# Pacing VectorE's side work in attention, and respacing scatters and gathers between expert blocks

## The chip, the cores and the metric

The kernel runs on one core of one Trainium2 chip, in fp32. The metric is the device time of one execution in microseconds, lower being better; a figure for a kernel is the median of its runs. The engines are called TensorE (PE; its weight loads are listed apart as PEld), VectorE (DVE), ScalarE (ACT), GpSimd (POOL) and SyncE (SP, which here only issues DMAs).

## The reference, cut to what matters

The input is a pair of images, 2 × 256 channels × 56 × 56 pixels, so 3136 tokens of 256 values in each batch. Layer 0 is a non-local convolution block without a softmax (a product of linear maps, folded into one 256 × 256 matrix), with a residual and a ReLU. Layer 1 is a transformer layer over the tokens:

```python
t = _to_tokens(x)
t = t + _L1_attn_ref(_ln_t(t), L1_attn_W_attn, L1_attn_W_proj)
t = t + _L1_ffn_ref(_ln_t(t), L1_ffn_gate_w, L1_ffn_gate_b, ...)
x = _from_tokens(t, x)
```

`_L1_attn_ref` is causal softmax attention with four heads of 64. `_L1_ffn_ref` sends every token to the best two of eight experts; an expert is 256 → 512, exact GELU, 512 → 256, and its output is weighted with the softmax value of the gate:

```python
top2_vals, top2_idx = jax.lax.top_k(probs, 2)
...
h = jax.nn.gelu(xf @ w1 + bb1, approximate=False)
y = h @ w2 + bb2
return (acc + we[:, None] * y, None)
```

## The kernel before

In time the kernel has four stages, which follow one another with some overlap: the convolution, attention of batch 0, attention of batch 1, and the expert blocks. Each engine works through its own list of instructions in the order in which the Python code issues them, so the order is written out by hand.

**Attention (`attend`).** A query block has W = 448 tokens; there are NB = 7 of them in a batch, and `hp` counts two pairs of heads. One step (b, i, hp, j) is one tile of 128 keys against a query block: scores on TensorE (L804), exp on ScalarE (L808) into a tile `st`, a mask on VectorE where the tile is cut by the diagonal (L811), and the sum of the exps on VectorE (L822, L827) into `acc`. The product of the exps with the values (L855) follows LAG = 3 steps later. After the last step of a query block ScalarE copies the finished product (L862) and POOL adds its two halves into `qT` (L863).

Two steps after that comes a *visit*. It issues the projections of the next queries, keys and values (L599, L613, L628), and the output projection of finished rows with its residual (`project_out`, L682 and L687). Then `sum_rows` (L866 to L890) turns the collected exps into row sums: eight matmuls (L876), a copy on ScalarE (L881) into `line`, and SP's DMAs (L884, L887) to memory and back. A list `later` of tasks with due steps holds what follows: `invert` 4 steps later (reciprocal L896 and DMAs L897, L902), `scale` 6 steps after that (L908, which multiplies the rows in `qT`), `hand_on` 2 steps after that.

All the rest of the work is cut into generators in a queue: the statistics of the second layer norm (`closer`, L177 and L178), the routing arithmetic, and the scatter of each token's normalized row to the slots of its two experts (copies L1493 and, for batch 1, L1499 on VectorE, then the indirect DMA L1501 on POOL, two per tile of 128 tokens). Within attention `between` (L2162) takes one piece from that queue in every step, except in the cut steps of the first query block:

```python
tick[0] += 1
if not cut or i:
    pull()
```

**Experts (`experts`).** There are 102 blocks of 128 rows. One turn of the loop issues: `hidden` (L1637 on TensorE, GELU L1646 on ScalarE), `inputs` of a later block (transposes L1614), `weights` (a copy of the expert's first matrix on VectorE, L1625), `outputs` of the block three earlier (L1656 on TensorE, L1666 on VectorE, then a DMA to `y_slots` L1671 or a scatter to `y_tokens` on POOL L1677), and last `between`, which is `meanwhile` (L2234). Every third turn the experts' numbers are read into registers of TensorE and VectorE (`experts_of`, L1517 to L1523). The first 57 blocks hold the rows of batch 0, the last of these mixed with rows of batch 1.

`meanwhile` counts turns and pulls pieces from the queue: 2 or 3 by turns while batch 1's scatters are being issued (`placed[1]` and not `sent[1]`), otherwise 4 or 2. When batch 0's outputs are complete, `written` (L2220) is called once: it makes three iota tiles on POOL (L2227) and queues `finish(0)` and `finish(1)`. `finish(0)` collects batch 0's result: two outputs per token from `y_slots` by indirect DMAs on POOL (L1834), added on VectorE (L1869), transposed on TensorE (L1883), copied on ScalarE (L1888) and stored (L1889). Its gathers are limited to 1 or 2 a turn:

```python
while gathered[0] == 1 + turn[0] % 2:
    yield False
```

Of the kernel before, what the change touches and what calls it, by code (L numbers as in the profile page):

```python
# [28 lines left out]
def conv_attn_moe_kernel(  # L29
# [481 lines left out]
    def layer1(nm, general):  # L511

        with ExitStack() as whole:
# [182 lines left out]
                    yield False  # L696

            unclosed = [NCH] * B

            def closer(b, first, m, k):  # L700

                for n in range(first, first + m):
                    stats(b, n, 1, k, bg, f"o{nm}{b}")
                    unclosed[b] -= 1
                    yield True

            def attend(qT, kT, v, fst, fs, psc, py, open_batch, visit, between, clock, later, finished):
# [156 lines left out]
                        del yps[b, hp, i]  # L864

                def sum_rows(b, hp, i):  # L866
                    yh = qT[:, hp, i * W : (i + 1) * W]
                    r = (b * NH + hp) * NB + i
                    sn = f"{nm}{b}_{hp}_{i}"
                    acc = accs[b, hp, i]  # L870
                    summed.add((b, hp, i))
                    sp = bank(f"sp_{b}_{hp}_{i}")

                    flat = acc.rearrange("p a w -> p (a w)")
                    for g in range(4):
                        nc.tensor.matmul(  # L876
                            sp[g * 32 : (g + 1) * 32, : W // 2], ones[:, :32],
                            flat[:, g * W // 2 : (g + 1) * W // 2], start=True, stop=True,
                        )
                    line = fs.tile([P, W], F32, tag="rb", bufs=3, name=f"line_{sn}")  # L880
                    nc.scalar.copy(line[:, : W // 2], sp[:, : W // 2])  # L881
                    halves = sum_d[r].rearrange("a (h w) -> (a h) w", h=2)
                    for g in range(4):
                        nc.sync.dma_start(  # L884
                            out=halves[g : g + 1], in_=line[g * 32 : g * 32 + 1, : W // 2]
                        )
                    nc.sync.dma_start(  # L887
                        out=sums[:, r], in_=sum_d[r].rearrange("a (p f) -> (a p) f", p=HS)
                    )
                    later.append((clock[0] + 4, invert, b, hp, i, yh))  # L890

                def invert(b, hp, i, yh):
                    r = (b * NH + hp) * NB + i
                    sn = f"{nm}{b}_{hp}_{i}"
                    back = fs.tile([P, 2 * W // P], F32, tag="back", name=f"back_{sn}")
                    nc.vector.reciprocal(back, sums[:, r])  # L896
                    nc.sync.dma_start(  # L897
                        out=inv_d[r].rearrange("a (p f) -> (a p) f", p=HS), in_=back
                    )
                    rb = fs.tile([P, W], F32, tag="rb", bufs=3, name=f"rb_{sn}")  # L900
                    for a in range(2):
                        nc.sync.dma_start(  # L902
                            out=rb[a * HS : (a + 1) * HS], in_=inv_d[r, a].partition_broadcast(HS)
                        )
                    later.append((clock[0] + 6, partial(scale, rb), b, hp, i, yh))

                def scale(rb, b, hp, i, yh):
                    nc.vector.tensor_tensor(yh, yh, rb, ALU.mult)  # L908
                    later.append((clock[0] + 2, hand_on, b, hp, i, yh))

                def hand_on(b, hp, i, yh):
# [2 lines left out]
                def due(now):  # L914
                    while later and (now is None or later[0][0] <= now):
                        _, task, b, hp, i, yh = later.pop(0)
                        task(b, hp, i, yh)
                        later.sort(key=lambda e: e[0])

                ends = {s[:2]: n for n, s in enumerate(steps)}  # L920
                LAG, BEHIND, FREED = 3, 2, 4
                visits = {BEHIND: (0, -1, NH - 1)}
# [4 lines left out]
                final = visits.pop(len(steps) + BEHIND)  # L927
                visits[len(steps) + 1] = final
                for n in range(len(steps) + LAG):
                    if n in visits:  # L930
                        visit(*visits[n])
                        b, i, hp = visits[n]
                        if i >= 0 and visits[n] != final:
                            sum_rows(b, hp, i)
                        aligned()
                    if n + 1 < len(steps) and n > LAG and steps[n][2] == 0 and steps[n - LAG - 1][2] == 0 and steps[n - LAG - 1][4]:
                        turn_rows(*steps[n][:2])
                    if n < len(steps):
                        b, i = steps[n][:2]
                        if n == 0 or steps[n - 1][0] != b:  # L940
                            open_batch(b)
                        between(b, i, ends[b, i] - n, (steps[n][3] + 1) * P > i * W + 1)

                    late = n >= LAG and steps[n - LAG][4]
                    if n >= LAG:
                        due(clock[0])
                        clock[0] += 1
                    if n >= LAG and not late:
                        values(n - LAG)
                    if n < len(steps):  # L950
                        scores(n)
                    if late:
                        values(n - LAG)
                sum_rows(final[0], final[2], final[1])
                return due

            def attend_general(b, qT, kT, v):
# [584 lines left out]
            def experts(w1s, w2s, b2s, ex, es, ps6, between, need, written, settle, decide):  # L1542


                LATE = 3
# [230 lines left out]
                for n in range(-1, MAIN + 1):  # L1776
# [11 lines left out]
                    for m in (n + 1, n + 2):  # L1788
                        if m < MAIN and m not in wb:
                            wb[m] = weights(m)  # L1790
                    if n == MAIN - 1:
                        decide()
                    for m in sorted(act):
# [18 lines left out]
                        ids.extend(experts_of(len(ids) // GB))  # L1812
                    between()

            def finish(b, oy, bufs):

                t = ts[b]

                def fetch(n, m, k):
# [8 lines left out]
                    ahead.append((n, m, k, ys, rows))  # L1828
                    for c, y in enumerate(ys):
                        for a in range(m):  # L1830
                            while gathered[0] == 1 + turn[0] % 2:
                                yield False
                            gathered[0] += 1
                            nc.gpsimd.indirect_dma_start(  # L1834
                                out=y[:k, a],
                                out_offset=None,
                                in_=y_slots,
                                in_offset=bass.IndirectOffsetOnAxis(
                                    ap=idxs[b][:k, c, n + a : n + a + 1], axis=0
                                ),  # L1840
                                bounds_check=MIXED * P - 1,
                                oob_is_err=False,
                            )
                            yield True
# [46 lines left out]
                        in_=ot[:, :, :w],  # L1891
                    )

                ahead, added = deque(), None
                parts = deque(pairs())
                if b:
                    parts = deque([(0, 1, P), *pairs(1, LAST)])
                while b == 0 and (parts or ahead):
                    if parts:
                        yield from fetch(*parts.popleft())  # L1900
                    if len(ahead) == bufs or not parts:
                        now = ahead.popleft()
                        yield from add(*now)
# [182 lines left out]
            else:  # L2086
# [54 lines left out]
                def visit(b, i, hp):  # L2141
# [20 lines left out]
                def between(b, i, left, cut):  # L2162
# [33 lines left out]
            with ExitStack() as moe:  # L2196
# [23 lines left out]
                def written():  # L2220
# [4 lines left out]
                    for a in range(GB):  # L2225
                        hots.append(hot.tile([P, REST], F32, name=f"hot{a}_{nm}"))
                        nc.gpsimd.iota(  # L2227
                            hots[a], pattern=[[1, REST]], base=LAST * P - OFF, channel_multiplier=0,
                            allow_small_or_imprecise_dtypes=True,
                        )  # L2230
# [25 lines left out]
                with tc.manual_schedule(engines={PE, DVE, POOL, SP, ACT}):  # L2256
                    experts(
                        first[0], w2s, b2s, ex, es, ps6,
                        meanwhile, need, written, settle, decide,
                    )  # L2260

    def late():
# [170 lines left out]
```

## Time and profile before

| | |
|---|---|
| three runs | 1254.31, 1254.82, 1254.89 us |
| median | 1254.82 us |
| the profiled execution | 1272.23 us, of which its span 1270.5 us |
| granted TensorE clock over the span | 0.995 |
| convolution | 0 to about 112 us |
| attention, batch 0 | about 112 to 470 us |
| attention, batch 1 | about 470 to 845 us |
| expert blocks | about 845 to 1271 us |

The profile was recorded in an execution of its own, 17.4 us longer than the median. Durations and positions below come from it. "Busy" is the time in which an engine executes an instruction; "issue" as a releaser means that the engine waited for nothing that the profile shows. VectorE's busy share over the span, in 40 slices from first to last, in tenths:

```profile
DVE  2683567566766575576677887785743433455664
```

It is highest in slices 19 to 28, which is attention of batch 1.

### The profile page before, as it was taken

The numbers are of one execution on the slowest core, as the hardware profiler recorded it, in microseconds if no ns is written. First come the engines' busy times: TensorE is split into PE (matmuls) and PEld (weight loads), VectorE is DVE, ScalarE is ACT, GpSimd is POOL, SyncE is SP. The second block draws the span as 40 slices with busy tenths as digits, with TensorE's granted clock in tenths as the row PEclk, the third lists the DMA queues.
The fourth block names the chain that finished last, engine by engine and source line by source line (L and its number), as shares of the span: only waits on it lengthen the run. The fifth ranks groups of instructions, "written<-read, shape, count | busy, mean of one in ns | idle before, by whom it ended". The sixth has DMA issues, their size and how long they took to land.

```text
span 1270.5 us, 28742 instructions
## 1 busy us (share of the span) xinstructions
PE 1247.3 (98%) x10881; PEld 857.1 (67%) x10881; DVE 773.9 (61%) x1687; ACT 613.1 (48%) x1237; POOL 356.2 (28%) x318
## 2 busy tenths in 40 slices
PE   8999999999999999999999999999999999999998
PEld 8876655555454645655555543469888999899996
DVE  2683567566766575576677887785743433455664
ACT  0255555565656565455555655563332333344442
POOL 1103231110021104211112766100266112666651
PEclk9999999999999999999999999999999999999999
DMA  9995101000000000100000223641344343466654
GB/s 314 354 345 187 25 23 37 25 15 26 14 17 16 7 20 17 36 21 14 9 16 25 71 67 110 202 136 61 101 135 151 101 114 101 142 200 200 212 164 125
DMA packets 118723, 125.66 MB, mean 99 GB/s; under 512 B 27223, under 2 KB 108488, under 8 KB 118578
## 3 DMA queue, kind: packets, MB, share of 16 engines
q1 hardware_dynamic: 107922, 97.19, 25.3%
q0 software_dynamic: 9840, 25.67, 6.0%
q8 instruction: 90, 1.47, 0.5%
q10 hardware_dynamic: 816, 0.88, 0.2%
q14 instruction: 55, 0.45, 0.1%
HBM read 62.06 MB, written 61.05 MB: 97 GB/s over the span
## 4 chain that ended last, share of the span: by engine, by line
PE 91%; DVE 4%; DMA 1%; issue 1%; ACT 1%; SPq 0%; DVEq 0%; ACTq 0%
PE sc_f L804 19%; PE yp_f L855 18%; PE ht_f L1637 14%; PE yp_f L1656 14%; PE qk_f L613 7%; PE v_f L628 4%; PE pp_f L682 3%; PE cp L410 3%; PE gram L317 2%; DVE acc_f L827 2%; PE tp_f L1614 2%; PE sp_f L876 1%; PE xp_f L599 1%; PE yo_f L1883 1%; DMA w1s_f<-in_w_dram 0%
## 5 line engine op out<-in xcount | busy, mean ns | idle before, releaser
L808 ACT ACTIVATE st_f<-sc_f 128x896 f32<-128x896 f32 (+5 forms) x400 | 330.7, 838 | 198.0 <-PE sc_f L804 178.9
L827 DVE TENSOR_TENSOR acc_f<-acc_f,st_f 128x896 f32<-128x896 f32 (+6 forms) x344 | 344.5, 1002 | 118.9 <-ACT st_f L808 109.1
L804 PE MATMUL sc_f<-qT_f,kT_f 64*64 64x448 f32 (+5 forms) x3136 | 347.5, 499 | 0.3 <-ACT st_f L808 0.3
L855 PE MATMUL yp_f<-st_f,v_f 64*64 64x448 f32 (+5 forms) x2928 | 328.0, 510 | 4.1 <-ACT acc_f L862 2.5
L804 PEld LDWEIGHTS sc_f<-qT_f,kT_f 64*64 64x64 f32 x3136 | 144.8, 133 | 128.9 <-issue 106.2
L1646 ACT ACTIVATE g_f<-ht_f,b1b 128x128 f32<-128x128 f32 x408 | 116.6, 371 | 227.3 <-PE ht_f L1637 123.4
L855 PEld LDWEIGHTS yp_f<-st_f,v_f 64*64 64x64 f32 x2928 | 125.1, 133 | 132.2 <-issue 99.3
L1637 PE MATMUL ht_f<-xT_f,w_f 128*128 128x128 f32 x1600 | 196.9, 276 | 5.2 <-issue 5.2
L1637 PEld LDWEIGHTS ht_f<-xT_f,w_f 128*128 128x128 f32 x1600 | 193.8, 192 | 9.1 <-issue 4.6
L1501 POOL DMA_INDIRECT x_slots<-xr_f,idx x100 | 120.4, 1204 | 147.0 <-DVE xr_f L1499 77.6
L863 POOL TENSOR_TENSOR qT_f<-acc_f 128x448 f32<-128x448 f32 x26 | 29.6, 1140 | 406.3 <-ACT acc_f L862 406.3
L1625 DVE COPY w_f<-w1s_f 128x1024 f32 x102 | 72.7, 713 | 90.0 <-PE ht_f L1637 34.2
L584 POOL TENSOR_SCALAR xn_f<-t 128x256 f32<-128x256 f32 (+1 forms) x50 | 82.4, 1655 | 129.4 <-DVE t L185 43.6
L1677 POOL DMA_INDIRECT y_tokens<-ys_f,to_f x57 | 59.2, 1038 | 125.2 <-DVE ys_f L1666 102.9
L613 PE MATMUL qk_f<-px_f,wat 128*128 128x512 f32 (+2 forms) x224 | 88.2, 546 | 0.6 <-ACT px_f L605 0.6
L1666 DVE TENSOR_TENSOR ys_f<-yp_f,kT_f 128x128 f32<-128x128 f32 x102 | 29.5, 289 | 92.3 <-PE yp_f L1656 69.5
L613 PEld LDWEIGHTS qk_f<-px_f,wat 128*128 128x128 f32 x224 | 40.6, 190 | 46.3 <-issue 41.7
L1656 PE MATMUL yp_f<-px_f,g_f 128*128 x204 | 62.3, 387 | 1.6 <-issue 1.6
L1656 PE MATMUL yp_f<-kT_f,g_f 128*128 x204 | 62.1, 386 | 0.0
L1656 PE MATMUL yp_f<-v_f,g_f 128*128 x204 | 61.8, 385 | 0.0
L1656 PE MATMUL yp_f<-w2s_f,g_f 128*128 x204 | 61.6, 384 | 0.0
L1834 POOL DMA_INDIRECT y_f<-y_slots,idx x50 | 55.5, 1110 | 17.1 <-issue 17.1
(299 smaller groups left out, 1302.4 us busy)
## 6 DMA issues: line engine op xcount, KB each, us to landing
x_slots<-fill SPq DMA_DIRECT2D x1, 8190.0 KB
xb_f<-x_slots SPq DMA_DIRECT2D x60, 130.0 KB
x_slots<-fill SPq DMA_DIRECT2D x1, 7296.0 KB
y_slots<-ys_f SPq DMA_DIRECT2D x57, 128.0 KB
kept<-t SPq DMA_DIRECT2D x2, 3200.0 KB
x<-in_x_dram SPq DMA_DIRECT2D x14, 448.0 KB
rb_f<-inverses SPq DMA_DIRECT2D x56, 112.0 KB
y_f<-y_tokens SPq DMA_DIRECT2D x23, 256.0 KB
```

What stands on the lines that cost most here:

```text
L584: nc.gpsimd.tensor_scalar(xn[:k, a], ts[b][:k, n + a, :C], ts[b][:k, n + a, MEAN : MEAN + 1], ts[b][:k, n + a, RSTD : RSTD + 1], ALU.subtr ...
L613: nc.tensor.matmul(ps[:, :w], wat[:, c, d0 : d0 + P], px[:, s % 2, c, :w], start=(c == 0), stop=(c == NH - 1),)
L804: nc.tensor.matmul(to, left, right, start=True, stop=True)
L808: nc.scalar.activation(st[rows, :, c0:], ps[rows, :, c0:W], AF.Exp, scale=SCALE)
L827: nc.vector.tensor_tensor(acc[rows, :, c0:], acc[rows, :, c0:], st[rows, :, c0:], ALU.add)
L855: nc.tensor.matmul(to, left, right, start=first, stop=end)
L1501: s = nc.gpsimd.indirect_dma_start(out=xds[b], out_offset=bass.IndirectOffsetOnAxis(ap=idxs[b][:kk, k, n : n + 1], axis=0), in_=xr[:kk], i ...
L1625: nc.vector.tensor_copy(w, w1s[:, :, bass.ds(e, 1), :].rearrange("p c e h -> p c (e h)"))
L1637: nc.tensor.matmul(ht[:, k, :], w[:, c, k * P : (k + 1) * P], xT[:, c, :], start=(c == 0), stop=(c == NH - 1),)
L1646: nc.scalar.activation(g[:, k, :], ht[:, k, :], AF.Gelu, bias=b1bs[b][:, k, i : i + 1])
L1656: nc.tensor.matmul(yp[:, :C], g[:, k, :], w2s[k][:, bass.ds(e, 1), :].rearrange("p e d -> p (e d)"), start=(k == 0), stop=(k == KH - 1),)
L1677: s = nc.gpsimd.indirect_dma_start(out=y_tokens, out_offset=bass.IndirectOffsetOnAxis(ap=to[:, n % GB : n % GB + 1], axis=0), in_=ys, in_o ...
```

## The change

It has five parts.

1. **A budget for VectorE's side work.** `room(n)` computes how much time of VectorE a step leaves: the step's length on TensorE, less the mask of a cut tile, less the sum. `between` adds that to `spare` and pulls a piece only if `spare` is above −0.8 (−0.9 while batch 0's rows are being scattered), for 0.35 (0.3). Each visit adds 2.0, up to 2.0, and pulls at 0.5 (0.8) each while more than 0.3 is there. Statistics cost another 0.25 and a scaling 0.6. The exception for cut steps of the first query block goes.
2. **The row sums' copy moves behind the values.** `sum_rows` keeps its matmuls and returns `store_sums`, which holds the copy L881 and the DMAs; it is called after `values` of the same step. `invert` and `scale` so come one step later. For the last query block of batch 1 `scale` comes 9 instead of 6 steps after `invert`.
3. **Batch 1's scatters.** While they are open, a new hook `amid`, called between `weights` and `outputs`, pulls one piece, and `meanwhile` pulls 1 or 2 instead of 2 or 3.
4. **The gathers of `finish(0)`.** There are none in its first two turns, one a turn in the next two, and after that two a turn, but one in every fourth.
5. **The iotas.** They are no longer issued together in `written`, but one by one between the first gathers.

```diff
                 for n in range(first, first + m):
                     stats(b, n, 1, k, bg, f"o{nm}{b}")
+                    spare[0] -= 0.25
...
-                    line = fs.tile([P, W], F32, tag="rb", bufs=3, name=f"line_{sn}")
+                    return partial(store_sums, b, hp, i, sp)
+
+                def store_sums(b, hp, i, sp):
+                    yh = qT[:, hp, i * W : (i + 1) * W]
+                    r = (b * NH + hp) * NB + i
+                    sn = f"{nm}{b}_{hp}_{i}"
+                    line = fs.tile([P, W], F32, tag="rb", bufs=3, name=f"line_{sn}")
...
-                    later.append((clock[0] + 6, partial(scale, rb), b, hp, i, yh))
+                    loading = b == B - 1 and i == NB - 1
+                    later.append((clock[0] + (9 if loading else 6), partial(scale, rb), b, hp, i, yh))
...
                     nc.vector.tensor_tensor(yh, yh, rb, ALU.mult)
+                    spare[0] -= 0.6
...
+                def room(n):
+
+                    _, i, _, j, first, _, _ = steps[n]
+                    off = j * P - i * W
+                    width = W - max(0, off)
+                    return (
+                        2 * 0.75 * width / W
+                        - (0.42 if off > -P else 0)
+                        - (0 if first else 0.07 + 1.02 * width / W)
+                    )
...
-                            sum_rows(b, hp, i)
+                            copy_sums = sum_rows(b, hp, i)
...
                         values(n - LAG)
+                    if copy_sums:
+                        copy_sums()
                     if n < len(steps):
                         scores(n)
...
+                    amid()
                     if n == MAIN - 1:
                         decide()
...
+            def number_columns(a):
+
+                nc.gpsimd.iota(
+                    hots[a], pattern=[[1, REST]], base=LAST * P - OFF, channel_multiplier=0,
+                    allow_small_or_imprecise_dtypes=True,
+                )
...
-                            while gathered[0] == 1 + turn[0] % 2:
+                            while gathered[0] == (1 if turn[0] < since + 4 else 2 - (turn[0] % 4 == 0)) or turn[0] < since + 2:
                                 yield False
...
-                ahead, added = deque(), None
+                ahead, added, since = deque(), None, turn[0]
+                steps = deque(range(GB))
...
                         yield from fetch(*parts.popleft())
+                        if len(parts) % 2 == 0 and steps:
+                            number_columns(steps.popleft())
...
+                    spare[0] = min(spare[0] + 2.0, 2.0)
+                    while spare[0] > 0.3:
+                        spare[0] -= 0.8 if placed[0] and not sent[0] else 0.5
+                        pull()
...
-                    if not cut or i:
+                    spare[0] = min(spare[0], 1.0) + room
+                    sending = placed[0] and not sent[0]
+                    if spare[0] > (-0.9 if sending else -0.8):
+                        spare[0] -= 0.3 if sending else 0.35
                         pull()
...
                     if placed[1] and not sent[1]:
-                        pull(2 + turn[0] % 2, every=True)
+                        pull(1 + turn[0] % 2, every=True)
...
+                def amid():
+                    if placed[1] and not sent[1]:
+                        pull(every=True)
```

More of the change, by code (lines that the diff above doesn't have):

```diff
@@ L698, in layer1 @@
             unclosed = [NCH] * B
+            spare = [0.0]
             def closer(b, first, m, k):
@@ L866, in sum_rows @@
                 def sum_rows(b, hp, i):
-                    yh = qT[:, hp, i * W : (i + 1) * W]
-                    r = (b * NH + hp) * NB + i
-                    sn = f"{nm}{b}_{hp}_{i}"
                     acc = accs[b, hp, i]
@@ L879, in sum_rows @@
                         )
+                    return partial(store_sums, b, hp, i, sp)
[3 more added lines that the diff above has]
+                    sn = f"{nm}{b}_{hp}_{i}"
                     line = fs.tile([P, W], F32, tag="rb", bufs=3, name=f"line_{sn}")
                     nc.scalar.copy(line[:, : W // 2], sp[:, : W // 2])
-                    halves = sum_d[r].rearrange("a (h w) -> (a h) w", h=2)
+                    split = sum_d[r].rearrange("a (h w) -> (a h) w", h=2)
                     for g in range(4):
                         nc.sync.dma_start(
-                            out=halves[g : g + 1], in_=line[g * 32 : g * 32 + 1, : W // 2]
+                            out=split[g : g + 1], in_=line[g * 32 : g * 32 + 1, : W // 2]
                         )
@@ L929, in attend @@
                 for n in range(len(steps) + LAG):
+                    copy_sums = None
                     if n in visits:
@@ L941, in attend @@
                             open_batch(b)
-                        between(b, i, ends[b, i] - n, (steps[n][3] + 1) * P > i * W + 1)
+                        between(b, i, ends[b, i] - n, (steps[n][3] + 1) * P > i * W + 1, room(n))
                     late = n >= LAG and steps[n - LAG][4]
@@ L953, in attend @@
                         values(n - LAG)
-                sum_rows(final[0], final[2], final[1])
+                sum_rows(final[0], final[2], final[1])()
                 return due
@@ L1540, in early_input, with experts @@
                 early_xT.append(xT)
-            def experts(w1s, w2s, b2s, ex, es, ps6, between, need, written, settle, decide):
+            def experts(w1s, w2s, b2s, ex, es, ps6, between, amid, need, written, settle, decide):
                 LATE = 3
@@ L2160, in visit, with between @@
                     ring.clear()
-                def between(b, i, left, cut):
+                    spare[0] = min(spare[0] + 2.0, 2.0)
+                    while spare[0] > 0.3:
+                        spare[0] -= 0.8 if placed[0] and not sent[0] else 0.5
+                        pull()
+                def between(b, i, left, cut, room):
                     if b == B - 1 and i == NB - 1 and left < NH * NCH - 2:
@@ L2224, in written @@
                     hot = pool(moe, "hot", bufs=1, side="right")
[L2225 to L2230, printed above, removed]
+                    hots.extend(hot.tile([P, REST], F32, name=f"hot{a}_{nm}") for a in range(GB))
                     queue.append(finish(0, oy, 2))
@@ L2258, in layer1 @@
                         first[0], w2s, b2s, ex, es, ps6,
-                        meanwhile, need, written, settle, decide,
+                        meanwhile, amid, need, written, settle, decide,
                     )
```

## The prediction

> **What bounds the kernel now.** I read five views in this order: the page's busy times and slices, the chain of waits, the windows by stage, the waits of TensorE, and its timeline where a wait is long. First the page:
>
> ```profile
> PE 1247.3 (98%) x10881; PEld 857.1 (67%) x10881; DVE 773.9 (61%) x1687; ACT 613.1 (48%) x1237; POOL 356.2 (28%) x318
> PE 91%; DVE 4%; DMA 1%; issue 1%; ACT 1%; SPq 0%; DVEq 0%; ACTq 0%
> L1501 POOL DMA_INDIRECT x_slots<-xr_f,idx x100 | 120.4, 1204 | 147.0 <-DVE xr_f L1499 77.6
> L1677 POOL DMA_INDIRECT y_tokens<-ys_f,to_f x57 | 59.2, 1038 | 125.2 <-DVE ys_f L1666 102.9
> L1834 POOL DMA_INDIRECT y_f<-y_slots,idx x50 | 55.5, 1110 | 17.1 <-issue 17.1
> ```
>
> TensorE is busy in 98% of the span and carries 91% of the chain. The change takes no matmul away, so only TensorE's holes and slow stretches can be won. The windows by stage (attention of batch 0, of batch 1, expert blocks; columns PE, weight load, DVE, ACT, POOL, clock, DMA share, GB/s):
>
> ```profile
> 112.00:470.00 358.00, 357.40 (x3552) 191.58 (x3550) 228.52 (x332) 206.59 (x309) 53.08 (x36) 1.00 0.08 21
> 470.00:845.00 375.00, 370.93 (x3723) 197.22 (x3717) 267.53 (x489) 212.49 (x316) 113.83 (x80) 1.00 0.20 59
> 845.00:1271.00 426.00, 411.00 (x2795) 380.37 (x2793) 220.00 (x676) 158.24 (x536) 169.26 (x161) 0.98 0.44 137
> ```
>
> The holes are 0.6, 4.1 and 15.0 us. The waits that name them (total, times, longest):
>
> ```profile
> PE ht_f L1637 <- issue: 5.2, 6, 1.1
> PE yp_f L855 <- ACT acc_f L862: 2.5, 4, 0.7
> ...
> PE yp_f L855 <- DVE st_f L811: 1.4, 3, 0.8
> ...
> PEld yp_f L855 <- DVE st_f L811: 7.4, 20, 1.6
> ```
>
> In attention they point at VectorE's mask (L811) and at the copy of a finished row block (L862); in the experts at no engine, only at "issue". The worst expert place in TensorE's timeline (start, length, matmuls, idle before):
>
> ```profile
> 914.85 1.28 PE L1637 MATMUL ht_f<-xT_f,w_f 128*128 128x128 f32 x10
> 916.74 0.40 PE L1637 MATMUL ht_f<-xT_f,w_f 128*128 128x128 f32 x2 [0.61 <-issue]
> 918.19 0.38 PE L1637 MATMUL ht_f<-xT_f,w_f 128*128 128x128 f32 x2 [1.06 <-issue]
> 919.61 0.59 PE L1637 MATMUL ht_f<-xT_f,w_f 128*128 128x128 f32 x2 [1.03 <-issue]
> ```
>
> and the windows around it and two like it:
>
> ```profile
> 910.00:920.00 10.00, 7.30 (x49) 6.90 (x49) 4.36 (x20) 1.09 (x5) 6.50 (x7) 0.96 0.49 160
> 920.00:930.00 10.00, 10.00 (x60) 8.85 (x60) 6.15 (x25) 3.79 (x15) 6.35 (x7) 0.87 0.37 108
> ...
> 980.00:990.00 10.00, 7.69 (x38) 6.44 (x38) 4.02 (x11) 3.53 (x14) 5.49 (x6) 0.83 0.41 144
> 1090.00:1100.00 10.00, 8.07 (x57) 7.50 (x57) 1.68 (x6) 1.40 (x5) 6.99 (x7) 1.00 0.52 156
> 1100.00:1110.00 10.00, 10.00 (x57) 8.99 (x57) 6.02 (x15) 5.00 (x19) 5.87 (x6) 0.83 0.37 110
> ```
>
> The reader is to see holes beside a POOL that issues indirect DMAs back to back (6.5 to 7 of 10 us), and a lowered clock right behind them.
>
> [...] clock means of 0.87, 0.83 and 0.83 follow the holes[...]. [...] batch 0 shows 0.6 us of holes, yet its stream has 13.8 us more than its matmuls back to back (below), so I work from starts. [...] The profiled execution took 1272.23 us, 1.7 more than its span and 17.4 more than the median of 1254.82: something in it is absent from plain runs.
>
> **Part 1, VectorE's side work paced.** The two batches have the same attention steps, but by the row durations batch 0 gives VectorE 33 us of side work and batch 1 72 us (statistics 0.42 + 0.18, row copies 0.42, scalings L908 0.62, routing). That is a twin experiment: from sum matmul (L876) to the next I subtract the interval's own matmuls at their usual spacing. What is left sums to 13.8 us in batch 0 and 19.9 in batch 1. So all of batch 1's heavier side work costs 6.1 us at most; that is the ceiling. Where it sits: 1.8 in 516.5 to 534.0 (17.53 against 14.83 of matmuls; twin excess 0.86), where three statistics pairs and one scaling (2.3 us) fall into four cut steps, which have a mask of 0.42 that TensorE waits for (one wait of 0.82 at 525.45); 1.8 after 764.9; 0.7 to 1 around 668 (0.7 beside router matmuls whose order stays); 0.5 each near 633 and 806. By the issue order, the changed kernel puts the pairs of the first place into the visit before it, which carries 4.0 us of side work instead of 2.3. Cover: VectorE idles 2.16 us at such a visit (before 161.44), and its first sum there may run late, since five st buffers stand behind a lag of three steps. Cost nothing; if the cover fails, 26 visits by 0.2 us lose 5. After 764.9 about 0.9 goes with L862, whose copy came late; another statistics-and-scaling pair still shares a step. I take 1.8 + 1.0 + 0.3 + 0.3 + 0.2 = 3.6 us won; bounds 0 and 6.1.
>
> **Part 2, the sums' copy a step later.** ACT's line copy (0.34) moves behind L862 and so ahead of the next two exps. Their scores now start 0.79 to 0.99 us after the exp that frees their bank, so 0.34 more still fits: nothing, and if the slack were gone 26 × 0.34 = 8.8 us lost. At eight small blocks the line copy ends within 0.1 us of L862's start: at most 0.8 gained, taken as 0. The five SP transfers, reciprocal and scaling come one step (1.50 us) later; projections read the rows only at a later visit, and SP issues nothing there that TensorE awaits within a step. The last block's first scaling is given three steps more; before, it waited 1.66 us for its transfer at 826 with TensorE undisturbed: nothing. For the last half, after attention, the wait is three blocks by either number.
>
> **Part 3, batch 1's scatters.** Meanwhile pulled 2 or 3 pieces a block, now 1 or 2, and one more between the weight copies and the outputs: 2.5 on average either way, so the 50 scatters finish in the same block. VectorE's copy (0.42 + 0.17) may now stand ahead of the two output sums (0.29 each) on DVE: those come 0.6 us later, in a block of 3.73 us with DVE busy 52% (220.0 of 426); cover is that the next output matmuls come a block later; without it 20 blocks × 0.3 = 6 lost. What it could win is the holes: about 8 us idle at four places (916, 932, 980, 1098) and about 1.7 behind three of them at half rate, 12.7 together. Each follows a register load (L1523) that TensorE does every third block, at 912, 928, 976 and 1093, with three to six indirect DMAs around it; but at least five other loads (941, 953, 964 among them) with four or five passed without a hole. Bounds −12.7 to +6. That the profiled run exceeds the plain one by 17.4 speaks for holes of the profiling, so I take 0.
>
> **Part 4, gathers.** Before: 1.5 a block from the start, 33 blocks for 50. After: none for two blocks, one for two, then 1.75 on average, 48 / 1.75 = 27.4, so 31 to 32 blocks of the 43 left. They end about two blocks earlier, hence nothing at the tail. But POOL then has 4 scatters and 7 gathers in four blocks: at the 1.33 us from issue to issue that rows back to back show, 14.6 of 14.9 us, where before 2.5 × 1.33 = 3.33 of 3.73 (89%) was used. I take 0; bounds 0 to +5.
>
> **Part 5, iotas.** Three of 0.695 us (1.95 from 1082.74) no longer stand together before the first gathers; POOL work moved, TensorE does not wait for it: 0.
>
> **Sum.** 3.6 us off the profiled 1272.2 gives about 1268.6; I carry the same 3.6 to plain runs, since they have the same steps: 1254.8 − 3.6 = 1251.2, rounded to 1251.
>
> **Rivals.**
> A, the forecast: attention 3 to 4.5 won, experts within 1: 1249.5 to 1252.5. For it: the twin difference and named mask waits. Against: eight of the thirteen intervals differ by under 0.4 us.
> B, the expert holes are real and spreading the DMAs breaks them: 4 to 9 more of the 12.7, so 1242 to 1247. For: each hole stands in a POOL burst. Against: bursts without holes, and the profiled run's surplus.
> C, the change moves work without effect: the visits become as long as the steps become short, and what pacing wins at 520 comes back at 600: 1253 to 1256. For: 91% of the chain is TensorE at work.
> D, the slower side: POOL becomes full in the gather stage. Deciding point: 14.92 / 11 = 1.356 us per indirect DMA; at 1.40, 11 × 1.40 = 15.4 overruns four blocks by 0.5, over 27 blocks 3.4 us, and y_tokens scatters (L1677) queued behind gathers hold the three ys buffers, thus the output sums and TensorE's banks. With holes at a fuller POOL up to 8: 1257.5 to 1262. For: 1.33 is 2% from the point. Against: POOL's row shows 125.2 us idle before L1677.
>
> **How the numbers follow.** A 0.45, B 0.25, C 0.15, D 0.15. Faster means by over 0.2%, 2.5 us, about what repeated runs can tell: below 1252.3. A lies there by five sixths: 0.38 + B 0.25 = 0.63; same 0.07 + C 0.15 = 0.22; slower 0.15. The range 1243 to 1258 leaves out B's lower end (0.05) and most of D (0.13). A alone: 1249.5 to 1252.5.
>
> **What would show it.** In the changed profile: no wait for L811 near 525 and fewer than 20 weight-load waits for it; L862 after 764.9 prompt; batch 1's excess at 16 to 17 us; the same batch 0 excess within 1 us. The exps after L862 about 0.3 later with no wait on sc_f. For B: no "issue" waits on L1637 and no clock mean under 0.95 in the experts, with the plain time going along. If those vanish in the profile and the plain time stays, they were the profiling's. For D: back-to-back POOL rows from about 1095, L1677 waiting for POOL itself, and TensorE waits on L1656. A plain time above 1254.8 with batch 1 shortened would make the expert parts, not pacing, the error.

## The result, and the profile after

The change takes 1.6 us off: 1253.18 us (22 runs, 1252.03 to 1254.29) against 1254.82 before (22 runs, 1253.89 to 1255.86), a ratio of 0.9987 with a 95% interval of 0.9982 to 0.9993. That is less than the forecast's 3.6, and lies within the bound of 0.2% that the prediction called no change. It falls into the range of rival C (1253 to 1256), not into that of the forecast's own case A (1249.5 to 1252.5).

The profiled execution of the changed kernel took 1253.73 us, of which its span 1252.0, so it is 0.5 us from the median. The page, busy times and then the chain of waits (which could be followed back only to about the middle of the execution this time):

```profile
PE 1238.6 (99%) x10881; PEld 852.3 (68%) x10881; DVE 775.2 (62%) x1687; ACT 614.0 (49%) x1237; POOL 348.5 (28%) x318
...
PE 48%; DVE 1%; issue 0%; ACT 0%; DVEq 0%
```

TensorE bounds the kernel as before. The windows by stage (columns as in the prediction):

```profile
112.00:470.00 358.00, 357.43 (x3551) 192.25 (x3551) 226.76 (x332) 206.32 (x309) 52.76 (x36) 1.00 0.07 21
470.00:845.00 375.00, 373.12 (x3758) 200.66 (x3751) 273.78 (x502) 214.51 (x324) 106.13 (x80) 1.00 0.20 59
845.00:1252.00 407.00, 400.28 (x2764) 372.29 (x2762) 217.13 (x665) 157.44 (x530) 169.58 (x160) 1.00 0.46 143
```

The expert stage has 6.7 us without TensorE instead of 15.0, at full clock. TensorE's waits in the changed kernel:

```profile
PE gram L317 <- DMA xr<-in_x_rows_dram: 3.4, 2, 3.2
PE yp_f L857 <- ACT acc_f L864: 1.7, 3, 0.6
...
PE yp_f L857 <- DVE st_f L813: 0.3, 1, 0.3
```

No "issue" wait is left, and the mask wait (L813 is L811 of before) has shrunk from 1.4 to 0.3. Read against the profile of before, this looks like 18.5 us won, of which 15.4 between the first and the last expert block. The plain runs say 1.6. The experiments had to find out which of the two profiles was not like its plain runs.

### The profile page after: what moved, and what is told of

The parts are those of the page before. It is cut to its first block, busy times and chain, and to the rows that moved or that the text cites. A ratio compares the mean times of both kernels' runs of the same rounds, so it can differ in the third digit from the quotient of the medians.

```text
span 1252.0 us, 28748 instructions
## 1 busy us (share of the span) xinstructions
PE 1238.6 (99%) x10881; PEld 852.3 (68%) x10881; DVE 775.2 (62%) x1687; ACT 614.0 (49%) x1237; POOL 348.5 (28%) x318
## 5 line engine op out<-in xcount | busy, mean ns | idle before, releaser
L1522 POOL DMA_INDIRECT x_slots<-xr_f,idx x100 | 113.5, 1135 | 139.2 <-DVE xr_f L1520 70.6
L1698 POOL DMA_INDIRECT y_tokens<-ys_f,to_f x57 | 59.3, 1040 | 122.0 <-DVE ys_f L1687 93.9
L613 PE MATMUL qk_f<-px_f,wat 128*128 128x512 f32 (+2 forms) x224 | 88.2, 546 | 0.6 <-ACT px_f L605 0.6
L1677 PE MATMUL yp_f<-px_f,g_f 128*128 x204 | 60.9, 380 | 0.0
L1677 PE MATMUL yp_f<-v_f,g_f 128*128 x204 | 60.7, 379 | 0.0
L1677 PE MATMUL yp_f<-w2s_f,g_f 128*128 x204 | 60.7, 379 | 0.0
L1677 PE MATMUL yp_f<-kT_f,g_f 128*128 x204 | 60.7, 379 | 0.0
```

The costliest lines, as they stand in the source:

```text
L613: nc.tensor.matmul(ps[:, :w], wat[:, c, d0 : d0 + P], px[:, s % 2, c, :w], start=(c == 0), stop=(c == NH - 1),)
L1522: s = nc.gpsimd.indirect_dma_start(out=xds[b], out_offset=bass.IndirectOffsetOnAxis(ap=idxs[b][:kk, k, n : n + 1], axis=0), in_=xr[:kk], i ...
L1677: nc.tensor.matmul(yp[:, :C], g[:, k, :], w2s[k][:, bass.ds(e, 1), :].rearrange("p e d -> p (e d)"), start=(k == 0), stop=(k == KH - 1),)
L1698: s = nc.gpsimd.indirect_dma_start(out=y_tokens, out_offset=bass.IndirectOffsetOnAxis(ap=to[:, n % GB : n % GB + 1], axis=0), in_=ys, in_o ...
```

## The experiments

The twelve experiments ran in five sets; all kernels of a set, and its runs of the kernel before, shared one chip. In two sets the kernel before took 1272.0 and 1271.2 us, in the other three 1254.5, 1254.7 and 1254.5. I call these the slow and the fast place. By the record the slow one was chip 3 (set 1) and chip 13 (set 3), the fast one chip 11 (set 2) and chip 4 (sets 4 and 5). No chip was seen as both, and for the profile of before and for the result the chip isn't recorded.

Two measures are used throughout. The *excess* is what the prediction defined: the time from one row-sum matmul to the next, less the interval's own matmuls at their usual spacing, summed over a batch. *Blocks 0 to 20* and so on are times from the start of one block's hidden matmuls to another's.

### Set 1, slow place: the change and its halves

`same` is the kernel before, unaltered.

> The kernel before, unaltered, timed and profiled anew. Theory 1 (the 15 us of holes in the expert blocks belong to that one profiled execution): plain time 1254.8, ratio 1.000, and this second profile has a span of about 1253 to 1257 without the holes behind the register loads near 916, 932, 980 and 1098. Rival (the holes belong to the kernel and the change removed them): the second profile shows them again, span near 1270.

`attn_only` has the change without its expert parts:

```diff
-                    amid()
...
-                            while gathered[0] == (1 if turn[0] < since + 4 else 2 - (turn[0] % 4 == 0)) or turn[0] < since + 2:
+                            while gathered[0] == 1 + turn[0] % 2:
...
-                        pull(1 + turn[0] % 2, every=True)
+                        pull(2 + turn[0] % 2, every=True)
```

with the iotas together again in `written`.

> Parts 1 and 2 alone, expert blocks as before. Theory 1 (the plain gain is the attention's, and the expert parts do nothing): 1253.2, like the whole change, 1.6 us under before; batch 1's attention 3.8 us shorter in the profile. Rival (attention gains the 4 us that the profiles show, and the expert parts give 2 back): about 1251.

`experts_only` has the change with the pulls of before, the row sums' copy at its old place and the last scaling after 6 steps:

```diff
-                            copy_sums = sum_rows(b, hp, i)
+                            sum_rows(b, hp, i)()
...
-                    if spare[0] > (-0.9 if sending else -0.8):
-                        spare[0] -= 0.3 if sending else 0.35
+                    if not cut or i:
                         pull()
```

> Parts 3, 4 and 5 alone, attention as before. Theory 1: 1254.8, ratio 1.000 within 0.0005. Rival (the expert parts cost what attention gains): about 1256.5 to 1257. Third (they are the gain): about 1253.2.

`whole` is the changed kernel.

> The whole change beside its halves on the same chip: 1253.2. If the halves add up, its difference to before is the sum of theirs within 0.6 us.

| | median us | ratio to before | 95% interval |
|---|---|---|---|
| before | 1271.98 | | |
| same | 1272.16 | 1.0000 | 0.9990 to 1.0010 |
| attn_only | 1270.19 | 0.9988 | 0.9978 to 0.9997 |
| experts_only | 1271.99 | 1.0006 | 0.9996 to 1.0017 |
| whole | 1271.45 | 0.9994 | 0.9983 to 1.0005 |

None of the expected absolute times came, because the place was another, and batch 1's attention is 1.1 us shorter in the profile of `attn_only` than in that of `same`, not 3.8. In differences, attention's parts alone take 1.8 us off the median (1.5 by the ratio), as theory 1 has it, and the rival's 4 us (0.9970) lies outside the interval. That the expert parts cost 2 us (1.0016) is only just inside theirs, and is left to set 5; that they are the gain (0.9987) lies outside. By the ratios the halves add up to `whole` (0.9988 × 1.0006 = 0.9994); by the medians they miss it by 1.2 us, more than the 0.6 that had been set. `whole` shows no gain clear of the noise at this place.

But the 1272 us are the median of plain runs: the surplus of 17.4 us that the profile of before had over its runs is not the profiling's. That profile is like this place: the new profile of `same` has such holes again (span 1269.4 us), as its rival foresaw. And, against that rival, the changed kernel has them here too. Its waits of TensorE at this place:

```profile
PE yo_f L1912 <- DVE y_f L1898: 3.8, 5, 1.3
PE ht_f L1658 <- issue: 3.7, 8, 1.0
...
PE yp_f L1677 <- issue: 0.9, 2, 0.5
PE tp_f L1635 <- issue: 0.7, 1, 0.7
PE sc_f L806 <- issue: 0.7, 2, 0.5
```

The first line is another thing: TensorE waits there for VectorE's sums of the gathered rows (0.6 us in `same`). The other four have no releaser. Three windows of the changed kernel here,

```profile
910.00:920.00 10.00, 7.66 (x51) 6.76 (x50) 4.41 (x20) 1.32 (x6) 5.77 (x6) 1.00 0.50 153
920.00:930.00 10.00, 10.00 (x69) 9.07 (x68) 4.84 (x21) 2.79 (x11) 7.41 (x8) 1.00 0.41 121
970.00:980.00 10.00, 9.05 (x58) 7.73 (x57) 3.20 (x11) 2.94 (x12) 5.98 (x7) 1.00 0.46 165
```

and in the profile that came with the result:

```profile
910.00:920.00 10.00, 10.00 (x69) 9.11 (x68) 6.62 (x28) 3.54 (x13) 7.87 (x8) 1.00 0.54 180
920.00:930.00 10.00, 10.00 (x70) 9.16 (x70) 4.89 (x17) 3.66 (x14) 7.56 (x9) 1.00 0.54 176
970.00:980.00 10.00, 10.00 (x73) 9.46 (x72) 5.00 (x17) 3.92 (x15) 4.15 (x4) 1.00 0.30 96
```

One program, one order of instructions: at the slow place TensorE lacks 2.3 and 1.0 us in two of the windows, and at the fast one nothing. The changed kernel's blocks 0 to 40 take 160.3 us at the slow place and 152.1 at the fast one, blocks 40 to 60, which have no burst of POOL's indirect DMAs, 74.6 at both. So it isn't the change that took the holes out.

At the slow place the expert parts do shift time, by one profile each, without a net gain. Blocks 60 to 80 take 80.5 and 81.9 us with them (`experts_only`, `whole`) and 83.9 and 84.2 without (`same`, `attn_only`; 82.3 in the profile of before), blocks 80 to the last 91.7 and 91.4 against 87.7 and 88.2 (88.6).

### Set 2, fast place: register loads, and each attention part by itself

`no_loads` takes the register loads out of the kernel before and gives every block a fixed expert:

```diff
-                return nc.values_load_multi_w_load_instructions(
-                    eblks[b][0:1, s : s + GB],
...
+                return [(r * GB + a) * E // MAIN for a in range(GB)]
```

> The kernel before without the register loads of expert numbers: every block takes a fixed expert (block number times 8 over 102), so the routed choice of weights is left out of the computation; all matmuls, copies and DMAs stay. Theory (on a chip where the kernel before takes 1272, the issue holes need the register load and the register-addressed weights that come with it, together with POOL's indirect DMAs): no wait on issue in the expert blocks above 0.3 us, full clock, about 1256. Rival (POOL's DMA bursts alone starve TensorE): the holes stay, 1268 or more. On a chip where the kernel before takes 1255 neither shows, and it stays within 2 us of it.

`pace_only` is `attn_only` with the row sums' copy at its old place and 6 steps for the last scaling; `copy_only` is `attn_only` with the pulls of before. Their edits are the two halves of the diff of `experts_only`.

> Part 1 alone, the pacing budget, with the row sums' copy and everything else as before. If pacing is what shortens batch 1's attention: TensorE's time over its own matmuls between the row-sum matmuls of batch 1 falls from 19.6 or 19.9 to 16 to 18.5, as in the whole change, with the mask wait near 525 gone. If the moved copy does it: it stays above 19.

> Part 2 alone, the row sums' copy behind the values and the late scaling, pulls as before. Pacing theory: excess of batch 1 stays at 19.3 to 20, the mask wait near 525 stays, exps behind the copied products start 0.3 us later without a wait of the scores. Rival: 16 to 18.5.

`no_loads` took 1254.41 against 1254.51, ratio 0.9998 (0.9990 to 1.0007): as foreseen for this place, it decides nothing there. `pace_only` took 1256.67 and `copy_only` 1253.39 in one execution each; these are read by their traces. The first number is not explained by its attention, which is 1.2 us shorter than that of before. Against `same3` below, its blocks 0 to 20 take 0.6 us more, and its span ends 21.1 us after the start of its last block's hidden matmuls instead of 19.4; why, I didn't follow further. So that pacing alone shortens attention is seen, that it alone shortens the execution is not.

The excess in batch 1, by the intervals that differ (start in us), with `same3` and `attn_plain` (its sums only) from the sets below; "after" is the changed kernel at the fast place:

```
interval from   same (slow)  same3 (fast)  copy_only  pace_only  after  attn_plain
516                2.70         2.70         2.18       2.16      1.65
608                1.14         1.14         1.14       1.14      1.29
633                1.51         1.52         1.52       1.24      1.32
668                2.16         2.15         2.16       2.48      2.11
732                1.66         1.66         1.54       1.49      1.42
764                3.20         1.11         1.11       1.11      1.11
batch 1, sum      19.62        17.60        16.89      16.66     16.04   16.04
batch 0, sum      13.79        13.77        13.67      13.53     13.53   13.52
```

Pacing alone wins 0.94 + 0.24 = 1.2 us, the moved copy alone 0.71 + 0.10 = 0.8, both 1.56 + 0.24 = 1.8. The bounds in the expectations of `pace_only` and `copy_only` came from the 19.6 and 19.9 of the slow place. At the fast place the kernel before itself has 17.60, so they decide nothing, and the differences to `same3` do: both parts work, and in the interval from 516 their gains add up (0.54 and 0.52, together 1.05). At 516 to 527 it can be read off. VectorE in `same3`:

```profile
524.16 0.42 DVE L177 BATCH_NORM_STATS2 st_of<-t 128x6 f32<-128x256 f32 x1
524.61 0.18 DVE L178 BATCH_NORM_AGGREGATE t<-st_of 128x2 f32<-128x6 f32 x1
524.71 0.60 DVE L908 TENSOR_TENSOR qT_f<-qT_f,rb_f 128x448 f32<-128x448 f32 x1
525.23 0.42 DVE L811 TENSOR_TENSOR st_f<-st_f,keep 128x256 f32<-128x256 f32 x1
```

and TensorE in it:

```profile
525.71 0.66 PE L855 MATMUL yp_f<-st_f,v_f 64*64 64x192 f32 x8 [0.82 <-DVE st_f L811]
```

The mask of a cut tile stands behind a statistics pair and a scaling, and the values wait 0.82 us for it. VectorE in `copy_only`, where the scaling comes a step later:

```profile
523.42 0.42 DVE L177 BATCH_NORM_STATS2 st_of<-t 128x6 f32<-128x256 f32 x1
523.88 0.18 DVE L178 BATCH_NORM_AGGREGATE t<-st_of 128x2 f32<-128x6 f32 x1
523.97 0.39 DVE L812 TENSOR_TENSOR st_f<-st_f,keep 128x256 f32<-128x256 f32 x1
524.40 0.69 DVE L828 TENSOR_TENSOR acc_f<-acc_f,st_f 128x512 f32<-128x512 f32 x1
525.01 0.62 DVE L913 TENSOR_TENSOR qT_f<-qT_f,rb_f 128x448 f32<-128x448 f32 x1
```

The scaling now stands behind the mask, and the wait is 0.30 (in `pace_only` it is the pair that has gone and the scaling that has stayed, and the wait is 0.28):

```profile
524.42 0.66 PE L856 MATMUL yp_f<-st_f,v_f 64*64 64x192 f32 x8 [0.30 <-DVE st_f L812]
```

In the changed kernel three statistics pairs stand before the cut steps, where VectorE has no exps to sum yet:

```profile
516.57 0.42 DVE L177 BATCH_NORM_STATS2 st_of<-t 128x6 f32<-128x256 f32 x1
...
518.08 0.18 DVE L178 BATCH_NORM_AGGREGATE t<-st_of 128x2 f32<-128x6 f32 x1
518.18 0.61 DVE L914 TENSOR_TENSOR qT_f<-qT_f,rb_f 128x448 f32<-128x448 f32 x1
519.62 1.11 DVE L829 TENSOR_TENSOR acc_f<-acc_f,st_f 128x896 f32<-128x896 f32 x1 [0.83 <-ACT st_f L810]
```

After that burst of the visit VectorE still idles 0.83 us before the first exp arrives, so the burst costs nothing. No mask waits behind a pair at 523.5 or 525.1, the next scaling stands behind the first of these masks, and the values follow without a wait for it, on VectorE and TensorE:

```profile
523.51 0.41 DVE L813 TENSOR_TENSOR st_f<-st_f,keep 128x256 f32<-128x256 f32 x1
...
524.57 0.62 DVE L914 TENSOR_TENSOR qT_f<-qT_f,rb_f 128x448 f32<-128x448 f32 x1
```

```profile
524.23 0.59 PE L857 MATMUL yp_f<-st_f,v_f 64*64 64x192 f32 x5
```

### Set 3, slow place: are the register loads the cause?

`same2` and `no_loads2` are `same` and `no_loads` again.

> The kernel before once more, since the first repeat took 1272 and a later call's runs of it 1254.5. Where this call's runs of the kernel before take 1255: span 1252 to 1254, no issue holes in the expert blocks, excess of batch 1's attention 17.9 (as no_loads has with the same attention), interval from 764 at 1.1. Where they take 1272: the profile of the first repeat again, about 15 us of holes.

> The same kernel without register loads of expert numbers (each block takes a fixed expert, so the routed choice of weights is left out). Where the kernel before takes 1272: if the holes need the register loads, 1256 with no issue waits above 0.3; if POOL's bursts alone make them, 1268 or more. Where it takes 1255: 1254.5 again, which decides nothing.

`same2` took 1272.11 against 1271.19 (ratio 0.9999, 0.9987 to 1.0010). `no_loads2` took 1266.51, ratio 0.9962 (0.9948 to 0.9976), 4.7 us less than before but some 12 more than at the fast place. In the traces the gain stands in blocks 0 to 20, which take 75.3 us against 79.2 in `same2`. TensorE's waits in it:

```profile
PE ht_f L1631 <- issue: 3.3, 5, 1.2
...
PE yp_f L1650 <- issue: 1.2, 2, 0.8
```

Neither theory hit the number. Holes remain without a single load in the expert blocks (at 916, 933, 959, 973 and 1093 us, each with two to four of POOL's indirect DMAs begun within the 4 us before it), so the loads are not needed for them; they, or the register-addressed weights, make them worse.

### Set 4, fast place: the kernel before without holes

`plain_gathers` changes the kernel before: plain transfers from fixed rows stand in place of POOL's 50 gathers, so the routed choice of rows is left out.

```diff
-                            nc.gpsimd.indirect_dma_start(
-                                out=y[:k, a],
...
+                            r = (2 * (n + a) + c) * P
+                            nc.sync.dma_start(out=y[:k, a], in_=y_slots[r : r + k])
```

> The kernel before with the 50 indirect gathers of batch 0's result (POOL) replaced by plain transfers of as many rows from fixed places (SP), so the routed choice of rows is left out there; batch 1's scatters and the register loads stay. Where the kernel before takes 1272: if POOL's indirect bursts are where TensorE starves, the issue holes near 1093 to 1130 go (blocks 60 to 80 in 78 instead of 84 us) while those near 916 to 985 stay, about 1264 to 1267. If it is the transferred amount or something else, blocks 60 to 80 stay at 82 to 84 and the time at 1271. Where it takes 1255: no holes to lose, 1254 to 1255.

> The kernel before beside it. Where it takes 1255 in this call: no issue holes in the expert blocks, batch 1's attention excess 17.9 with 1.1 in the interval from 764. Where it takes 1272: about 15 us of holes, as in the two repeats, with blocks 60 to 80 in 82 to 84 us.

Both were at the fast place: `plain_gathers` 1255.16, ratio 1.0002 (0.9993 to 1.0010), `same3` 1254.84. So POOL's gathers cost nothing here; whether they are the cause of the slow place's holes after 1090 was not tried there. The value of this set is `same3`, the profile of before that belongs with its plain time. TensorE's waits in it:

```profile
PE yp_f L855 <- ACT acc_f L862: 1.7, 3, 0.6
PE yp_f L855 <- DVE st_f L811: 1.2, 2, 0.8
```

There is no "issue" wait. Against it the changed kernel reads as follows:

```
                          same3    after
span                     1253.6   1252.0
excess, batch 0            13.77    13.53
excess, batch 1            17.60    16.04
blocks 0 to 20             74.8     74.8
blocks 20 to 40            77.4     77.4
blocks 40 to 60            74.6     74.6
blocks 60 to 80            78.4     77.9
blocks 80 to the last      87.3     87.8
```

Attention is 1.8 us shorter, the 102 expert blocks take 392.5 us in both, what lies before the first row sum and behind the start of the last block is 0.3 longer, the span is 1.5 shorter before rounding, and the medians differ by 1.64. That closes the account. One part of the 1.8 isn't the change's: the interval from 804 has 0.12 us less than in `same3`, but with attention as before it took 36.38, 36.50 and 36.78 us in three profiles of this place (`plain_gathers`, `same3`, `no_loads`), and takes 36.38 in the changed kernel. Without this scatter pacing, the moved copy and both bring 1.1, 0.7 and 1.7 us instead of 1.2, 0.8 and 1.8.

### Set 5, fast place: the attention parts alone

`attn_plain` is `attn_only` with the edit of `plain_gathers`.

> Parts 1 and 2 with the experts' parts undone, and the 50 indirect gathers of batch 0's result replaced by plain transfers from fixed places (the routed choice of rows is left out there). Where the kernel before takes 1255, plain gathers change nothing, so this measures the attention parts: 1252.9 to 1253.2, ratio 0.9986 (the whole change's 1.6 to 1.8 us), and 1254.8 if the gain is elsewhere. Where it takes 1272: against the 1270.2 of the attention parts with indirect gathers, 1263 to 1266 if POOL's bursts are where TensorE starves (blocks 60 to 80 in 78 instead of 84 us), 1269 to 1271 if not.

It took 1253.17 against 1254.48, ratio 0.9987 (0.9980 to 0.9993), which is the whole change's ratio, as expected; its excess is 16.04 and its blocks 60 to 80 and 80 to the last take 78.4 and 87.3, as in `same3`. So the gain is in parts 1 and 2, and parts 3 to 5 add nothing beyond that interval.

## Why the prediction was right or wrong

**The mechanism of part 1 was right, its size three times too large.** The term was 1.8 + 1.0 + 0.3 + 0.3 + 0.2 = 3.6 us for pacing, with 0 for part 2. Pacing alone shortened attention by 1.2 us, both parts by 1.8. Measured at the fast place with both: 1.05 at 516 (not 1.8), nothing at 764 (not 1.0), 0.04 at 668, 0.20 at 633, nothing at 806 that isn't scatter, 0.24 in batch 0, which had been left out, and 0.24 at 732, less 0.15 lost at 608. The step that failed is the sizing by twins: all that batch 1's stream has over batch 0's was taken for VectorE's side work ("all of batch 1's heavier side work costs 6.1 us at most"). The twins differ in more than side work. In the interval from 764, 2.1 us of excess belongs to the slow place on which that profile was taken. TensorE there, in the profile `same`:

```profile
768.80 0.61 PE L855 MATMUL yp_f<-st_f,v_f 64*64 64x448 f32 x4 [0.71 <-ACT acc_f L862]
```

and in `same3`, the same instructions at the fast place:

```profile
767.90 1.31 PE L855 MATMUL yp_f<-st_f,v_f 64*64 64x448 f32 x12
```

The forecast did see that L862 came late there, and put it down to side work all the same. At the slow place the changed attention does take less in this interval (40.0 and 40.1 us in `attn_only` and `whole`, 40.7 to 41.5 with attention as before), but 1.0 more in the one before it (33.5 against 32.5); at the fast place it takes 39.4 either way. On `same3` the ceiling is 17.60 − 13.77 = 3.8 us, and of the 1.8 that the interval from 516 has over its twin, 0.8 remains in the changed kernel.

**The cover for the longer visits held.** Weight-load waits for the mask fell from 18 (6.7 us) in `same3` to 5 (1.6 us), and batch 0 got no longer. The forecast's sign of fewer than 20 is a weak one, since `same3` meets it too; the mask wait near 525 that is gone and batch 1's excess of 16.04 are the signs that count.

**Part 2 costs nothing, as worked out, but isn't worth nothing.** The exps behind L862 come 0.24 us later, and the scores still start 0.54 us or more after the exp that frees their bank. What I left out is that the scaling, one step later, leaves the place ahead of a mask. The part brings 0.8 us alone, of which 0.52 is that one wait, and 0.6 us on top of pacing (1.8 − 1.2).

**Parts 3, 4 and 5 at 0 were right**, in part by luck, for one reason was wrong: "that the profiled run exceeds the plain one by 17.4 speaks for holes of the profiling". The holes are in plain runs at the slow place, 17 us of them, and absent from every profile of the fast one. The forecast's sign "If those vanish in the profile and the plain time stays, they were the profiling's" came true, and what it was to show is false, for by their likeness the profile after is of the fast place and the one before of the slow one. The value 0 fits because the plain time of before came from the fast place. Rival B was thus right that the holes are real, and wrong that spreading the DMAs breaks them: the changed kernel has them at the slow place. Rival D did not come: in the changed kernel L1698 (L1677 of before) waited 93.9 us for VectorE's sums and 7.0 on issue, so POOL kept up at the fast place. At the slow one, TensorE's wait for the gathered sums (3.8 us in `whole` and 2.6 in `experts_only`, 0.6 in `same` and 1.4 in `attn_only`) and the longer blocks 80 to the last speak for a cost of D's kind.

**Rival C** has the number but not the reason: where it saw the gain come back, in the interval from 608, only 0.15 us did. The measured 1253.18 is the forecast's mechanism at half its size, and not side work moved without effect.

**What stays open** is the cause of the holes. That they stand in POOL's bursts is seen; that these make them was not shown, since a burst was never removed at the slow place. The DMA queues' instruction packets do not explain them: of the 18 gaps over 0.5 us between TensorE's starts in the expert blocks of `same`, one has such a packet in flight. Whether the place is the chip, or a condition that chips pass through, is open too. The expert half of the slow place's difference between `attn_only` and `whole` (0.9988 and 0.9994) lies within their intervals.

## What to carry to other kernels

Before a hole in a profile is priced, compare the profiled execution's time with the plain runs that the forecast is measured against: where they are apart by more than the runs' own spread, the profile may be of another condition, and its holes are suspects: those without a named releaser first, but here one that had a name (L862 after 764.9) was of the other place too. A twin stage is a good ceiling only for what the twins have in common, so look at each interval and at who is named as releaser there before adding it in. And where an engine serves both short operations that TensorE waits for and long ones that nobody does, moving the long ones by one step can bring two thirds as much as a scheduler for all of them (0.8 and 1.2 us of attention here).

## What the hardware showed unexpectedly

The same instructions took about 1254.5 us on chips 4 and 11 and 1271.2 to 1272.0 us on chips 3 and 13, in plain runs as in profiles. TensorE's starts stall there: in the expert blocks of `same` 18 times over 0.5 us pass from one start to the next, 13.0 us in all, against once and 0.5 us in `same3`. Only a part of that counts as idle (8.8 of the 15.8 us between the two spans). Most of these stalls have no named releaser and stand beside indirect DMAs of POOL, while the lengths of these DMAs (1.0 us in the median) and the distance from one to the next (1.31 and 1.32 us in the median where back to back) were the same at both places.

The clock is not the main part of it. It was 0.992 to 1.000 over the span at the slow place and 0.998 to 1.000 at the fast one. Leaving out the last 6 us of each span, the profile of before has TensorE at a granted clock of 0.50 three times, for 3.4 us each (from 919.2, 984.0 and 1100.1 us), at the end of a run of stalls or right behind it; `same` has one such stretch, and `attn_only`, whose span is 1268.0 us all the same, has none (0.999 over the span). I estimate from these stretches a loss of 5 us in the first and 1.7 in the second. At the fast place the profile after has none, and the clock over the span is 0.998 or 0.999 in all seven profiles.
